# Loads, clears and a bias in the opening stage of a four-layer graph network: x is loaded after the edges' ends, one clear is written at another place, and layer 0's bias is added on DVE

## Chip, core and metric

The kernel runs on one core of a Trainium2 chip. The metric is the device time of one execution in microseconds (us). Three runs of the kernel before gave 7706.85, 7705.21 and 7698.37 us; the median is 7705.21. All profile numbers come from one further execution that the hardware profiler recorded, of 7696.22 us.

## What is computed

A graph has 6250 nodes with 128 features in `x` and 100,000 edges with ends `src` and `dst`, sorted by `dst`. Four layers are applied one after the other, each to a normalised and clipped copy of `x`, and each result is added to `x`. Only layer 0 is touched by the change:

```python
h = jnp.maximum(_layernorm(x, axis=-1), 0.0)
x = x + _L0_gnn_ref(h, edge_index, ...)
# inside layer 0
h = x @ W_w + W_b
row, col = (edge_index[0], edge_index[1])
e = h[row] @ a_src + h[col] @ a_dst + a_b
e = jax.nn.leaky_relu(e, negative_slope=0.01)
attention = jax.nn.softmax(e, axis=0)
out = jax.ops.segment_sum(attention * h[col], row, num_segments=N_NODES)
```

Layers 1 to 3 (a mean over edges, two graph attentions, three edge convolutions) use the same edges and follow later.

## The kernel before, in words

The nodes are held as 49 tiles of 128 rows, the edges as tiles of 128 that are taken in chunks of 512. `tile_gnn_stack` is the opening stage. It ends with a flag (L253) and a branch on it (L255); the fast side of the branch, `stack`, runs the four layers. Nothing of `stack` starts ahead of the branch, so the opening stage and the layers lie one behind the other.

The opening stage has two strands that share the engines:

- **The edges' strand** (L137 to L253). `d_i` and `s_i` are the edges' ends as integers, loaded by L138 on the SP queue and L140 on the ACT queue. DVE turns them into differences, window offsets and masks that are stored to DRAM (`neg_d`, `mk_d`, L189 to L197). PE transposes three of them and DVE copies the results to `srcE`, `dstE`, `endE` (L211, L212). Then 98 steps count how often each node tile occurs: DVE makes a one-hot block `oh` (L230, three buffers), PE adds it up in `pc` (L233), and after each of four parts DVE reduces `pc` to `cnt` and to some limits in `ext` (L236 to L246).
- **The nodes' strand** (`node_steps`, L279 to L357). It is a generator; L235 calls its next step behind each of the 98 counting steps, and L247 runs what is left. It loads the weight `wx`, the bias `bx` and the two halves `av` of the attention vector (L290 to L297, all on the ACT queue), and appends to `wx` and `bx` two columns, their products with `av` (L308, L309). Then each node tile passes through three calls: `norm` (statistics for seven tiles at a time on DVE, L316, L317; a square root on ACT, L319; two small DVE steps, L320, L321; then ACT normalises, L329, PE transposes to `nt`, L331, and ACT copies, L333), `project` (PE: the product with `wx`, L338, and a product of a row of ones with the one-row `bx`, L339, which adds the bias in the accumulator `np`, two buffers) and `keep` (ACT copies `np` to `ev`, four buffers, L345, and its last column to `s_tab`, L346; the SP queue stores `ev` to the table `T0`, L347).

`x` itself is loaded in seven pieces at the top, on the ACT queue (L122 to L124). `clear_rows` (L261 to L269) fills places of a DRAM array with a constant, in two DMAs, one of 9360 KB and one of 195 KB, on the SP queue; for the first part, `rows_d[0]`, it is called at L304, in the nodes' second step. Layer 0's scatters to `rows_d[0]` (L1259) come after the branch.

The code is written in a layer that reorders instructions when the program is built: it keeps data dependencies and decides itself in which order each engine and each DMA queue gets its instructions. Each queue then issues strictly in that order. DMAs from SP and ACT take turns on eight completion semaphores, and a DMA waits until the one that used its semaphore eight DMAs earlier has landed.

Of the kernel before, what the change touches and what calls it, by code (L numbers as in the profile page):

```python
# [8 lines left out]
F32 = mybir.dt.float32  # L9
# [3 lines left out]
OP = mybir.AluOpType  # L13
# [4 lines left out]
P = 128  # L18
N = 6250
NT = 49  # L20
# [8 lines left out]
D = 128  # L29
# [59 lines left out]
def tile_gnn_stack(ctx: ExitStack, tc: tile.TileContext, a: dict, out: bass.AP):  # L89
# [5 lines left out]
    nc = tc.nc  # L95
    V = nc.vector
    const = ctx.enter_context(tc.tile_pool(name="shared", bufs=1))
    ident = const.tile([P, P], F32, name="ident")
# [7 lines left out]
    ones = const.tile([P, P], F32, name="ones")  # L106
# [5 lines left out]
    sh = dict(ident=ident, iof=iof, pid=pid, ones=ones, ones_tail=ones_tail, srcE=srcE, endE=endE)  # L112
# [6 lines left out]
    sh["mk_d"] = mk_d  # L119

    x = const.tile([P, NT, D], F32, name="x")
    xr = a["x"].rearrange("(i p) f -> p i f", p=P)  # L122
    for i in range(0, NT, 7):
        nc.scalar.dma_start(x[:, i:i + 7, :], xr[:, i:i + 7, :])  # L124
    sh["x"] = x
    sh["T0"] = dram.tile([NP, D + 1], F32, name="T0")
    sh["s_tab"] = const.tile([P, NT], F32, name="s_tab")
# [4 lines left out]
    with ExitStack() as st:  # L132
        one = st.enter_context(tc.tile_pool(name="pre", bufs=1))
        work = st.enter_context(tc.tile_pool(name="prew", bufs=3))
        ps = st.enter_context(tc.tile_pool(name="prep", bufs=2, space=PSUM))
        node = node_steps(nc, tc, a, sh, st)
        d_i = one.tile([R, 1024], I32, name="d_i")  # L137
        nc.sync.dma_start(d_i, a["dst"].rearrange("(r j) -> r j", j=1024))  # L138
        s_i = one.tile([R, 1024], I32, name="s_i")
        nc.scalar.dma_start(s_i, a["src"].rearrange("(r j) -> r j", j=1024))  # L140
        edge_i = one.tile([R, 2], I32, name="edge_i")
        V.memset(edge_i[:, 0:1], -1)
        V.memset(edge_i[:, 1:2], 1 << 20)
        dcol = bass.AP(tensor=a["dst"].tensor, offset=a["dst"].offset + 1023,
                       ap=[[1024, R - 1], [1, 1]])
        nc.sync.dma_start(edge_i[1:R, 0:1], dcol)
        dcol = bass.AP(tensor=a["dst"].tensor, offset=a["dst"].offset + 1024,
                       ap=[[1024, R - 1], [1, 1]])
# [41 lines left out]
        for m, src in enumerate((slob, dwb, neg)):  # L190
            for c, at, lo, hi in ((1, 256, 0, 256), (2, 0, 256, 768), (3, 0, 768, 1024)):
                nc.sync.dma_start(bass.AP(tensor=mk_d.tensor,
                                          offset=mk_d.offset + (3 * c + m) * 512 + at,
                                          ap=[[2 * 3 * 512, R], [1, hi - lo]]), src[:, lo:hi])
# [29 lines left out]
        for s in range(len(CAP)):  # L224
            t0, t1 = seg_tiles(s)
            pc = ps.tile([P, 8, NT], F32, name="pc")
            for t in range(t0, t1, 8):
                n = min(8, t1 - t)
# [5 lines left out]
                                 stop=t + 8 >= t1)  # L234
# [26 lines left out]
def clear_rows(nc, rows, none, s):  # L261

    for b0, nb, few in ((0, NT - 1, FEW[s][0]), (NT - 1, 1, FEW[s][1])):
        n = (CAP[s] - few) // P
        nc.sync.dma_start(bass.AP(tensor=rows.tensor, offset=rows.offset + (b0 * CAP[s] + few) * RW,
                                  ap=[[n * RW, P], [CAP[s] * RW, nb], [1, n * RW]]),
                          none[:, None, :n, :].rearrange("p o n f -> p o (n f)")
                          .to_broadcast([P, nb, n * RW]))


def no_rows(nc, pool):

    none = pool.tile([P, 4, RW], F32, name="none")
    nc.vector.memset(none, 0.0)
    nc.vector.memset(none[:, :, D:D + 1], -BIG)
    return none


def node_steps(nc, tc, a, sh, st):  # L279


    V, S = nc.vector, nc.scalar
    x, ident, ones = sh["x"], sh["ident"], sh["ones"]
    one = st.enter_context(tc.tile_pool(name="nd", bufs=1))
    w = st.enter_context(tc.tile_pool(name="ndw", bufs=3))
    ps = st.enter_context(tc.tile_pool(name="ndp", bufs=2, space=PSUM))

    wx = one.tile([P, D + 2], F32, name="wx")
    bx = one.tile([1, D + 2], F32, name="bx")
    nc.scalar.dma_start(wx[:, :D], a["L0_gnn_W_w"])  # L290
    b0 = a["L0_gnn_W_b"]
    nc.scalar.dma_start(bx[:, :D], bass.AP(tensor=b0.tensor, offset=b0.offset, ap=[[0, 1], [1, D]]))
    avs = []
    for j, half in ((0, 1), (1, 0)):
        v = a["L0_gnn_a_w"][half * D:(half + 1) * D, :]
        av = one.tile([P, D], F32, name=f"av{j}")
        nc.scalar.dma_start(av, bass.AP(tensor=v.tensor, offset=v.offset, ap=[[0, P], [1, D]]))  # L297
        avs.append(av)
    eps = one.tile([P, 1], F32, name="eps")
    V.memset(eps, LN_EPS)  # L300
    none = no_rows(nc, one)
    live = {}
    yield
    clear_rows(nc, sh["rows_d"][0], none, 0)  # L304
    for j, av in enumerate(avs):
        for t, n in ((wx, P), (bx, 1)):
            pr = one.tile([n, D], F32, name=f"pr{n}")
            V.tensor_tensor(pr, t[:, :D], av[:n, :], OP.mult)  # L308
            V.tensor_reduce(t[:, D + j:D + j + 1], pr, AX.X, OP.add)  # L309
    yield  # L310

    def stats(g):
        mv = w.tile([P, 7, 2], F32, name="mv")
        for i in range(7):
            s = w.tile([P, 6], F32, name="st")
            V.bn_stats(s, x[:, 7 * g + i, :])  # L316
            V.bn_aggr(mv[:, i, :], s)  # L317
        r = w.tile([P, 7, 2], F32, name="r")
        S.activation(r[:, :, 0], mv[:, :, 1], AF.Sqrt, bias=eps, scale=1.0)  # L319
        V.reciprocal(r[:, :, 0], r[:, :, 0])  # L320
        V.scalar_tensor_tensor(r[:, :, 1], mv[:, :, 0], -1.0, r[:, :, 0], op0=OP.mult, op1=OP.mult)  # L321
        return r

    def norm(i):
        if i % 7 == 0:
            live["r"] = stats(i // 7)
        r = live["r"]
        h = w.tile([P, D], F32, name="h")
        S.activation(h, x[:, i, :], AF.Relu, bias=r[:, i % 7, 1:2], scale=r[:, i % 7, 0:1])  # L329
        pt = ps.tile([P, P], F32, name="nt", bufs=1)  # L330
        nc.tensor.transpose(pt, h, ident)  # L331
        h1 = w.tile([P, P], F32, name="h1")
        S.copy(h1, pt)  # L333
        live[i] = h1

    def project(i):
        pp = ps.tile([P, D + 2], F32, name="np")
        nc.tensor.matmul(pp, live.pop(i), wx, start=True, stop=False)  # L338
        nc.tensor.matmul(pp, ones[0:1, :], bx, start=False, stop=True)  # L339
        live[i] = pp  # L340

    def keep(i):
        pp = live.pop(i)
        ev = w.tile([P, D + 1], F32, name="ev", bufs=4)
        S.copy(ev, pp[:, :D + 1])  # L345
        S.copy(sh["s_tab"][:, i:i + 1], pp[:, D + 1:])  # L346
        nc.sync.dma_start(sh["T0"][i * P:(i + 1) * P, :], ev)  # L347

    for i in range(NT + 2):
        if i < NT:  # L350
            norm(i)
        yield
        if 0 <= i - 1 < NT:
            project(i - 1)
        if 0 <= i - 2 < NT:
            keep(i - 2)
        yield  # L357


# [2008 lines left out]
```

## Time and profile before

| What | Value |
|---|---|
| median of 3 runs | 7705.21 us |
| profiled execution, its span | 7696.22 us, 7694.4 us |
| granted PE clock, mean over the span | 0.902 |
| busy: PE, DVE, ACT, POOL | 6191.9, 4916.1, 2115.0, 5303.9 us |
| opening stage: flag written | 168.39 us after the span's start |
| first DVE work of `stack` | 170.41 us |
| DMA in the first 40 us | 13.76 MB, mean 344 GB/s |

An engine's line in a list of instructions in order of time gives the start, the time of one (or of a merged run, with the count behind an x), engine, line, operation, output and input, and in brackets how long the engine was idle before it and what ended that. SPq and ACTq are DMA issues on the queues of those two engines. PEld is the loading of PE's stationary operand. Times of neighbouring instructions overlap a little, so a pace is read from the distance of two starts. A float32 product takes two passes, and each is counted as an instruction.

### The profile page before, as it was taken

What the parts mean: (1) busy time and instruction counts of PE and PEld (TensorE: products, weight loads), DVE (VectorE), ACT (ScalarE), POOL (GpSimd) and SP (SyncE); (2) the same over time, 40 slices, a digit from 0 to 9 for tenths busy, and PEclk for the clock granted to TensorE, in tenths of its full rate; (3) what the DMA queues carried; (4) which work ended last, traced back from release to release, by engine and by line L of the source; (5) the groups of instructions that cost most, each with busy time, mean ns of one, the idle gap of its engine ahead of it and who ended that gap; (6) DMA issues with size and microseconds to landing.
All of it is one profiled execution on the core that took longest, in us unless ns stands there. A gap on an engine that the chain in (4) does not pass through costs nothing.

```text
span 7694.4 us, 109942 instructions
## 1 busy us (share of the span) xinstructions
PE 6191.9 (80%) x35616; PEld 4418.6 (57%) x35616; DVE 4916.1 (64%) x15100; ACT 2115.0 (27%) x5081; POOL 5303.9 (69%) x5487
## 2 busy tenths in 40 slices
PE   6778886777777999996777777878778887777877
PEld 4677875555555666664554544555555555555554
DVE  5677886444446999995666666555555555555555
ACT  2134556222222222222111123222222222222222
POOL 0777772777776666654777755777767777677776
PEclk7778997999998999998888889999989999899999
DMA  3855763333336455433333324444434444333333
GB/s 121 258 162 168 216 189 124 93 92 93 92 87 133 142 144 146 143 104 95 88 89 93 89 79 125 122 126 122 126 114 123 125 122 126 110 119 118 117 118 108
DMA packets 778747, 954.40 MB, mean 124 GB/s; under 512 B 232584, under 2 KB 552494, under 8 KB 777942
## 3 DMA queue, kind: packets, MB, share of 16 engines
q1 hardware_dynamic: 555332, 519.06, 23.3%
q0 software_dynamic: 187680, 411.54, 18.5%
q10 hardware_dynamic: 35154, 16.67, 0.8%
q8 instruction: 289, 4.73, 0.3%
q14 instruction: 292, 2.39, 0.1%
HBM read 809.79 MB, written 137.02 MB: 123 GB/s over the span
## 4 chain that ended last, share of the span: by engine, by line
PE 39%; DMA 25%; POOL 13%; issue 9%; DVE 9%; ACT 2%; SPq 0%; POOLq 0%; DVEq 0%; ACTq 0%
DMA gb<-TB,srcE 13%; POOL gb L391 6%; PE pa L2011 5%; PE pz L2263 5%; DMA gl<-TLb,srcE 4%; PE pa L2290 4%; DMA g<-T,srcE 3%; PE pm L1892 3%; POOL gl L391 3%; DMA rows_d<-rw,pos 3%; PE pt L2251 3%; POOL g L391 3%; PE pb L2276 2%; PE pt L2253 2%; PE bank L1409 2%
## 5 line engine op out<-in xcount | busy, mean ns | idle before, releaser
L391 POOL DMA_INDIRECT gb<-TB,srcE x2346 | 2246.1, 957 | 859.6 <-issue 650.5
L2265 DVE TENSOR_TENSOR_SCAN sc<-mk,sc,pz 128x512 f32<-128x512 bf16 x585 | 748.4, 1279 | 1123.2 <-PE pz L2263 1123.2
L391 POOL DMA_INDIRECT gl<-TLb,srcE x782 | 783.5, 1002 | 364.4 <-issue 183.2
L391 POOL DMA_INDIRECT gl<-TL,srcE x782 | 754.4, 965 | 360.7 <-issue 153.8
L391 POOL DMA_INDIRECT g<-T,srcE x782 | 740.8, 947 | 357.5 <-issue 165.8
L2253 PE MATMUL pt<-ident,gb 128*128 128x128 f32 x2346 | 487.2, 295 | 608.0 <-DMA gb<-TB,srcE 597.3
L1259 POOL DMA_INDIRECT rows_d<-rw,pos x782 | 776.8, 993 | 251.8 <-issue 174.1
L2253 PEld LDWEIGHTS pt<-ident,gb 128*128 128x128 f32 x2346 | 315.2, 142 | 1051.8 <-DMA gb<-TB,srcE 772.9
L2256 ACT ACTIVATE z<-pt 128x512 f32<-128x512 f32 (+1 forms) x588 | 350.4, 596 | 1678.8 <-PE pt L2253 1571.3
L1897 ACT COPY mT<-pm 128x512 f32<-128x512 f32 (+1 forms) x588 | 343.7, 585 | 1399.0 <-PE pm L1894 1279.5
L1894 PEld LDWEIGHTS pm<-ident,gl 128*128 128x128 f32 x2346 | 317.9, 148 | 634.6 <-issue 318.2
L1892 PE MATMUL pm<-oh,wr 128*128 128x512 f32 (+1 forms) x1176 | 655.7, 641 | 31.6 <-DMA oh<-in_edge_weight 16.1
L2263 PE MATMUL pz<-z,wo 128*128 128x512 f32 (+1 forms) x1176 | 670.4, 655 | 0.0
L2290 PE MATMUL pa<-en,row 128*128 128x128 f32 x4692 | 669.0, 289 | 0.0
L2290 PEld LDWEIGHTS pa<-en,row 128*128 128x128 f32 x4692 | 624.2, 207 | 0.1
L1894 PE MATMUL pm<-ident,gl 128*128 128x128 f32 x2346 | 429.0, 290 | 239.9 <-DMA gl<-TLb,srcE 238.8
L2251 PE MATMUL pt<-oh,wr 128*128 128x512 f32 (+1 forms) x1176 | 612.5, 603 | 0.5 <-DVE ev L2157 0.5
L1898 DVE SCALAR_TENSOR_TENSOR lT<-mT,pm 128x512 f32<-128x512 f32 (+1 forms) x588 | 390.7, 675 | 286.1 <-ACT mT L1897 276.7
L2282 DVE TENSOR_SCALAR en<-iof,endE 128x128 f32<-128x128 f32 x2346 | 550.1, 301 | 0.0
L2276 PEld LDWEIGHTS pb<-ident,sc 128*128 128x128 f32 x2346 | 324.6, 153 | 357.9 <-issue 355.8
L2278 ACT COPY row<-pb 128x512 f32<-128x512 f32 (+1 forms) x588 | 344.1, 585 | 503.9 <-PE pb L2276 502.9
L2011 PE MATMUL pa<-px,oe 128*128 128x260 f32 x1564 | 407.7, 400 | 17.5 <-ACT px L2002 17.5
(346 smaller groups left out, 11735.5 us busy)
## 6 DMA issues: line engine op xcount, KB each, us to landing
mk<-mk_d SPq DMA_DIRECT2D x192, 1024.0 KB
mk<-mk_d SPq DMA_DIRECT2D x96, 512.0 KB
rows<-rows_d SPq DMA_DIRECT2D x98, 390.0 KB
gb<-TB,srcE POOLq DMA_INDIRECT x2346
wr<-TA SPq DMA_DIRECT2D x141, 256.0 KB
rows_d<-none SPq DMA_DIRECT2D x3, 9360.0 KB
ea<-in_edge_attr SPq DMA_DIRECT2D x195, 128.0 KB
wr<-TR SPq DMA_DIRECT2D x47, 448.0 KB
```

The source lines that it names most:

```text
L391: nc.gpsimd.indirect_dma_start(out=dst, out_offset=None, in_=table, in_offset=bass.IndirectOffsetOnAxis(ap=idx, axis=0),)
L1259: ins = nc.gpsimd.indirect_dma_start(out=rows_d[s], out_offset=bass.IndirectOffsetOnAxis(ap=idx, axis=0), in_=src, in_offset=None)
L1892: nc.tensor.matmul(pm[:, c0 * P:], wr[:, fb], oh[:, c0 * P:], start=True, stop=False)
L1894: nc.tensor.matmul(pm[:, c * P:(c + 1) * P], gl[:, c, fb], ident, start=False, stop=c == 3, is_transpose=True)
L2011: nc.tensor.matmul(pg, oe[:, c, :], px[:, c, :], start=c == c0, stop=c == 3)
L2251: nc.tensor.matmul(pt[:, c0 * P:], wr, oh[:, c0 * P:], start=True, stop=False)
L2253: nc.tensor.matmul(pt[:, c * P:(c + 1) * P], gb[:, c, :], ident, start=False, stop=c == 3, is_transpose=True)
L2263: nc.tensor.matmul(pz[:, c0:], wo[conv], z[:, c0:], start=True, stop=True)
L2265: V.tensor_tensor_scan(sc[:, c0:], masks.pop(k)[1][:, c0:], pz[:, c0:], 0.0 if carry[0] is None else carry[0][:, 511:512], OP.add, OP.max)
L2276: nc.tensor.transpose(pb[:, c, :], sc[:, c * P:(c + 1) * P], ident)
L2282: V.tensor_scalar(en[:, c, :], iof, endE[:, t:t + 1], None, op0=OP.is_equal)
L2290: nc.tensor.matmul(pa, row[:, c, :], en[:, c, :], start=c == c0, stop=c == 3)
```

## The change

Three edits, all ahead of the branch:

1. The seven loads of `x` are written behind the loads of `d_i` and `s_i`, still on the ACT queue.
2. The call that clears the places of the first part is taken out of the nodes' second step and written in the loop over the node tiles, at i = 14.
3. The bias `bx` becomes a block of 128 equal rows (loaded by a DMA that repeats the row). The product of ones with `bx` is gone; DVE adds `bx` to `np` and writes `ev`, now with 130 columns. ACT still copies the last column to `s_tab`, now from `ev`. The products with `av` are made for `bx` on 128 rows in place of one.

```diff
@@ tile_gnn_stack
     x = const.tile([P, NT, D], F32, name="x")
-    xr = a["x"].rearrange("(i p) f -> p i f", p=P)
-    for i in range(0, NT, 7):
-        nc.scalar.dma_start(x[:, i:i + 7, :], xr[:, i:i + 7, :])
     sh["x"] = x
...
         s_i = one.tile([R, 1024], I32, name="s_i")
         nc.scalar.dma_start(s_i, a["src"].rearrange("(r j) -> r j", j=1024))
+        xr = a["x"].rearrange("(i p) f -> p i f", p=P)
+        for i in range(0, NT, 7):
+            nc.scalar.dma_start(x[:, i:i + 7, :], xr[:, i:i + 7, :])
@@ node_steps
-    bx = one.tile([1, D + 2], F32, name="bx")
+    bx = one.tile([P, D + 2], F32, name="bx")
     nc.scalar.dma_start(wx[:, :D], a["L0_gnn_W_w"])
     b0 = a["L0_gnn_W_b"]
-    nc.scalar.dma_start(bx[:, :D], bass.AP(tensor=b0.tensor, offset=b0.offset, ap=[[0, 1], [1, D]]))
+    nc.scalar.dma_start(bx[:, :D], bass.AP(tensor=b0.tensor, offset=b0.offset, ap=[[0, P], [1, D]]))
...
-    clear_rows(nc, sh["rows_d"][0], none, 0)
     for j, av in enumerate(avs):
-        for t, n in ((wx, P), (bx, 1)):
-            pr = one.tile([n, D], F32, name=f"pr{n}")
-            V.tensor_tensor(pr, t[:, :D], av[:n, :], OP.mult)
+        for t in (wx, bx):
+            pr = one.tile([P, D], F32, name="pr")
+            V.tensor_tensor(pr, t[:, :D], av, OP.mult)
             V.tensor_reduce(t[:, D + j:D + j + 1], pr, AX.X, OP.add)
...
-        nc.tensor.matmul(pp, live.pop(i), wx, start=True, stop=False)
-        nc.tensor.matmul(pp, ones[0:1, :], bx, start=False, stop=True)
+        nc.tensor.matmul(pp, live.pop(i), wx, start=True, stop=True)
...
-        ev = w.tile([P, D + 1], F32, name="ev", bufs=4)
-        S.copy(ev, pp[:, :D + 1])
-        S.copy(sh["s_tab"][:, i:i + 1], pp[:, D + 1:])
-        nc.sync.dma_start(sh["T0"][i * P:(i + 1) * P, :], ev)
+        ev = w.tile([P, D + 2], F32, name="ev", bufs=4)
+        V.tensor_tensor(ev, pp, bx, OP.add)
+        S.copy(sh["s_tab"][:, i:i + 1], ev[:, D + 1:])
+        nc.sync.dma_start(sh["T0"][i * P:(i + 1) * P, :], ev[:, :D + 1])
...
             keep(i - 2)
+        if i == 14:
+            clear_rows(nc, sh["rows_d"][0], none, 0)
         yield
```

More of the change, by code (lines that the diff above doesn't have):

```diff
@@ L282, in node_steps @@
     V, S = nc.vector, nc.scalar
-    x, ident, ones = sh["x"], sh["ident"], sh["ones"]
+    x, ident = sh["x"], sh["ident"]
     one = st.enter_context(tc.tile_pool(name="nd", bufs=1))
```

## The prediction, made before the changed kernel ran

> **What bounds the kernel now.** I read the chain that ended last first, then the list in order of time up to 171 us, then the table by stretches, the groups of the opening stage, and the built order of both programs.
>
> Chain that ended last, shares of the span by engine:
>
> ```profile
> PE 39%; DMA 25%; POOL 13%; issue 9%; DVE 9%; ACT 2%; SPq 0%; POOLq 0%; DVEq 0%; ACTq 0%
> ```
>
> No engine bounds the whole. But the flag (168.39) and the branch cut the span in two, and all edits lie ahead of the cut, so the opening stage is read by itself. What is saved there moves the rest earlier. In the built programs every engine and queue has the same instructions in the same order behind the branch.
>
> The list in order of time, three stretches of the opening stage:
>
> ```profile
> 5.95 0.40 SPq L265 DMA_DIRECT2D rows_d<-none  x1
> ...
> 32.20 0.69 DVE L186 TENSOR_SCALAR slo<-s_i 98x1024 int32<-98x1024 int32 x1 [12.37 <-DMA s_i<-in_src]
> ...
> 41.37 0.82 ACTq L297 DMA_DIRECT2D av<-in_L_gnn_a_w  x2
> 44.40 0.29 DVE L308 TENSOR_TENSOR pr<-wx,av 128x128 f32<-128x128 f32 x1 [9.60 <-DMA av<-in_L_gnn_a_w]
> ...
> 54.20 0.55 DVE L230 TENSOR_TENSOR oh<-iob,hi 128x392 bf16<-128x392 bf16 x1
> ...
> 142.56 0.51 PE L233 MATMUL pc<-oh,ones_b 128*128 128x392 bf16 x1
> 142.86 0.42 PE L331 MATMUL nt<-ident,h 128*128 128x128 f32 x1
> 143.07 0.64 PE L338 MATMUL np<-wx,h 128*128 128x130 f32 x2
> 143.64 0.80 PE L339 MATMUL np<-bx,ones 1*128 1x130 f32 x2
> 144.37 0.51 PE L233 MATMUL pc<-oh,ones_b 128*128 128x392 bf16 x1
> ...
> 152.75 0.31 ACT L319 ACTIVATE r<-mv,eps 128x7 f32<-128x7 f32 x1
> ```
>
> First DVE waits 12.37 us for `s_i`, which ACT's queue issued behind `x`, and 9.60 us for `av`. Behind that second wait, in DVE's order, stand the copies of `srcE` and all one-hots, so counting starts at 54.20. Then comes the loop over nodes and counts. The starts give PE's pace: pc 0.30, nt 0.21, np 0.57, the bias product 0.73.
>
> The table by stretches (start:end, length, then busy us of PE, PEld, DVE, ACT, POOL, and the granted PE clock):
>
> ```profile
> 80.00:100.00 20.00, 19.97 (x65) 13.40 (x65) 9.22 (x31) 8.89 (x41) 0.00 (x0) 0.50 0.15 41
> 140.00:160.00 20.00, 19.37 (x63) 12.35 (x63) 11.18 (x39) 9.59 (x39) 0.00 (x0) 0.50 0.10 28
> ```
>
> PE fills the loop, at half the clock, and DVE is idle nearly half of it. The square roots (one for seven tiles) start at 57.34 and lastly 152.75: six periods in 95.4 us, 15.9 each. PE's own share of one is 14 counts, 7 transposes, 7 products, 7 bias products: 4.2 + 1.5 + 4.0 + 5.1 = 14.8.
>
> **The change, part by part.**
>
> *The clear.* It does not move. In SP's built order the DMA of 9360 KB is the fifth in both programs, ahead of `neg_d`; only the one of 195 KB goes, from ahead of the stores of `T0` to behind the fourth. I cost this at nothing: it issues in 0.39 us on a queue that has a store each 2 us. And the load of the first `av` still waits for the big clear, whose semaphore it takes over (41.37 is when the clear has landed). Ahead of that the same bytes flow (13.76 MB in 40 us), whichever comes first.
>
> *`x` behind `s_i`.* `s_i` goes first on ACT's queue, beside `d_i`, which DVE reads at 6.70. So the wait of 12.37 us goes. DVE's work up to the first `pr` (10.23 to 19.8, then the five steps of 32.20 to 34.8, then the copies and casts of 45.4 to 54.2) is some 21 us from 10.2, and ends near 31. What is late next is `av`, at 44.40 as before: DVE stands still for 13 us. From there it is 9.8 us ahead, for the first one-hot no longer has the copies between itself and `av`. It gives some back: two statistics that stood at 6.30 now stand here, the products with `av` too (eight steps at 0.2, from 44.40 to 45.40), and two more one-hots ahead of the square root. Counted along the built order, the two small steps L320 and L321 end at 53.0, where before L321 started at 59.66. **A = -6.7** (bounds: 0, should `av` land later by as much; -9.8). The loads of `x` end before 41 and hide under the wait for `av`; without that cover the first statistics would wait for them.
>
> *The bias product goes from PE:* 49 times 0.73 = 35.8 us of an engine that fills the loop. What is left of PE in a period is 9.7 us.
>
> *The add goes to DVE:* 49 times 128x130 from the accumulator. The nearest row is layer 0's last table:
>
> ```profile
> L1530 DVE TENSOR_TENSOR ev<-pp,b1a x49: 252/284/292, 1230.4 to 1319.4; 128x128 f32<-128x128 f32 x49
> ```
>
> 0.284 us; in a run one step starts 0.07 before the last ends (six one-hots of 0.554 take 2.94), so 0.22. A period on DVE: 14 one-hots at 0.49, 7 pairs of statistics at 0.26 (starts 79.98, 80.24), 7 adds, 0.2 for r: 10.4, and a seventh of four `cnt` blocks of 0.9: **10.9 us, more than PE's 9.7.** ACT loses 49 copies of 0.268; it was no bound.
>
> *The new wait.* The add waits for np, and behind it on DVE stand one-hots, which PE counts next; before, this wait was ACT's. I walked one period along the built order, from the start of a block of seven statistics (0): r is ready at 3.8, the first transpose runs at 4.45, the first np ends at 5.83, the next at 7.27, 8.4, 9.5, 10.6. DVE, which reaches its adds at 5.5, 6.7, 8.7, 9.9 and 11.0, stands still for 0.5 and 0.8 us at the first two and not at the others. The next block starts at 11.7; with `cnt`, **12.2 a period**. Bounds: 10.9 with no standing still, and 15.6 if each add waits as ACT's copy of np does now (its group: 33.2 us idle before 49 copies, 0.68 each, 4.7 a period). I take 12.2, since the wait in between is on two engines that are then near balance. Six periods: 73.2 in place of 95.4. **B = -22.2** (-30.0 to -1.8).
>
> *The tail.* From L321 of the last group to the flag is 14.7 us now (153.65 to 168.39), filled by PE. In the walk the last np ends 9.5 after r, and 0.75 later the flag. **C = -4.5** (0 to -6). The store of the last `ev` lands behind it as now: the layers' first DVE step came at 170.41, released by it.
>
> Sum: -6.7 - 22.2 - 4.5 = **-33.4 us**. On the profiled execution's own time, 7696.22, that is 7663; this execution lies 9 us under the median of the three runs, 7705.21, from which I get **7672**. The ends of all terms together: -46 and -2.
>
> **The rivals.** About 0.2%, 15.4 us here, is what a measurement of this kernel can tell from no change.
>
> 1. *PE gets its full clock.* From 77 to 79 us it had it: a count took 0.33 in place of 0.51, np 0.40 in place of 0.64. Then PE's period halves, DVE's 10.9 is all, and the gain is 6.7 + 30 + 6, some 43: 7662. Against it: in the loop the clock stayed at 0.50 from 80 us on, with PE busy 97%; a less busy PE gives no reason for more. The Trainium skill (TensorE: Matmul & The Clock Gate, Part 1) says that sustained activity releases a gated clock within some 3.4 us. By that rule the loop would have run at full clock already, the bias product would be worth about half, and the sum would be nearer -20; the trace disagrees, at 0.50 for 100 us. Chance 0.10.
> 2. *The two engines interlock.* Each add that waits holds up one-hots, PE then lacks counts, and the period becomes 14: -6.7 - 11.4 - 3 = -21, 7684. For it: both engines are strictly in order and near balance, with only three one-hot and two np buffers. Chance 0.17.
> 3. *A wait takes the place of the product.* The adds wait as long as ACT's copies did, 15.6, and `av` lands a few us later because `x` now flows beside the clear: -2 to -12, about 7699. This is also what is left if only the moved bytes count and the rest does not do what it says, as the clear shows. Chance 0.12.
> 4. *Slower, by the clock behind the branch.* PE has 39% of the chain, 3001 us, at a mean granted clock of 0.902. If the shifted start brings it 1% lower (0.893), PE's part costs 30 us and the gain is gone; at 0.887 it is slower by 17 us, about 7722. It decides from 0.892 on. Against it: three runs, each with its own phase, lie within 8.5 us. Chance 0.08.
>
> My forecast, periods of 11.3 to 13.2 us, gains 27 to 39 us: chance 0.53.
>
> **How the numbers follow.** The likeliest case gives 7672. The range goes from 7655 (rival 1, with the 7 us by which the fastest of the three runs lies under the median) to 7699 (rival 3 at its middle). That leaves out rival 4 and half of rival 3, 0.14, and little below. Faster by over 0.2%: the forecast and rivals 1 and 2, 0.80. Within: rival 3, 0.12. Slower: 0.08.
>
> **What would show it.** In the profile after: DVE's wait for `s_i` gone and one of some 13 us for `av` in its place, still ended near 44; the first one-hot at 45; the big clear still issued near 6 us; square roots 12.2 us apart; DVE busy 17 of 20 us in the loop and PE less than now; idle time of DVE before `ev`, released by np, of under 2 us a period; the flag near 135. Wrong would be: `av` landing at another time (A), periods over 14 (B), or a flag at 135 with an unchanged total (rival 4: then the time behind the flag has grown).

## The result, and the profile after

Five runs of the changed kernel gave a median of 7667.68 us (7662.97 to 7673.48). Five runs of the kernel before on the same chip gave 7702.68 (7698.03 to 7706.85). The ratio is 0.9954, with a 95% interval from 0.9943 to 0.9966: 35 us faster. The profiled execution of the changed kernel took 7662.97 us (span 7661.1, mean granted clock 0.907). So the time came out 4 us under the forecast of 7672.

In kernel.py of the changed kernel some lines have other numbers: the square root is L317 (before L319), the product with `wx` L336 (L338), the add that writes `ev` L342, the store of `T0` L344 (L347).

First the chain that ended last, shares of the span by engine:

```profile
PE 37%; DMA 23%; POOL 16%; issue 12%; DVE 9%; ACT 2%; SPq 0%; DVEq 0%; POOLq 0%; ACTq 0%
```

As before, no engine bounds the whole, and the answer lies in the opening stage. The same list in order of time as before (start, time of one, engine, line, operation, and in brackets the idle time before it with what ended that):

```profile
6.20 0.40 SPq L265 DMA_DIRECT2D rows_d<-none  x1
7.90 0.68 DVE L186 TENSOR_SCALAR slo<-s_i 98x1024 int32<-98x1024 int32 x1
...
42.58 0.82 ACTq L296 DMA_DIRECT2D av<-in_L_gnn_a_w  x2
45.76 0.29 DVE L306 TENSOR_TENSOR pr<-wx,av 128x128 f32<-128x128 f32 x1 [15.59 <-DMA av<-in_L_gnn_a_w]
45.98 0.56 DVE L230 TENSOR_TENSOR oh<-iob,hi 128x392 bf16<-128x392 bf16 x1
...
101.11 0.64 PE L336 MATMUL np<-wx,h 128*128 128x130 f32 x2
101.79 0.29 DVE L342 TENSOR_TENSOR ev<-np,bx 128x130 f32<-128x130 f32 x1 [0.73 <-PE np L336]
102.41 0.64 PE L336 MATMUL np<-wx,h 128*128 128x130 f32 x2
103.09 0.29 DVE L342 TENSOR_TENSOR ev<-np,bx 128x130 f32<-128x130 f32 x1 [0.53 <-PE np L336]
104.25 0.29 DVE L342 TENSOR_TENSOR ev<-np,bx 128x130 f32<-128x130 f32 x1
105.34 0.39 PE L336 MATMUL np<-wx,h 128*128 128x130 f32 x2
105.40 0.29 DVE L342 TENSOR_TENSOR ev<-np,bx 128x130 f32<-128x130 f32 x1
...
121.92 0.30 ACT L317 ACTIVATE r<-mv,eps 128x7 f32<-128x7 f32 x1 [2.59 <-DVE mv L315]
132.14 0.16 DVE L253 CAST flag<-pf 128x1 int32<-128x1 f32 x1 [0.48 <-PE pf L252]
134.05 0.49 DVE L274 MEMSET none<- 128x520 f32 x1 [1.75 <-DMA T<-ev]
```

The wait for `s_i` is gone (7.90). One wait for `av` of 15.59 us stands in its place, and the first one-hot follows it at once, at 45.98 in place of 54.20. In the loop, from 78 us on, DVE stands still before the first two adds of each new group of seven tiles (0.73 and 0.53 us here) and before none of the later ones. The flag comes at 132.14.

The table by stretches (start:end, length, busy us of PE, PEld, DVE, ACT, POOL with instructions, the granted PE clock, then the DMA share and GB/s):

```profile
60.00:80.00 20.00, 14.15 (x56) 7.35 (x55) 17.50 (x70) 9.97 (x38) 0.00 (x0) 0.78 0.17 50
80.00:100.00 20.00, 13.53 (x58) 7.12 (x57) 18.88 (x75) 8.52 (x35) 0.00 (x0) 0.84 0.14 40
100.00:120.00 20.00, 16.29 (x67) 9.65 (x68) 17.61 (x63) 10.73 (x41) 0.00 (x0) 0.78 0.15 42
```

The engines have changed places: DVE is now full to 17.5 to 18.9 of 20 us, PE to 13.5 to 16.3. And the granted clock, 0.50 in these stretches before (from 80 us on), is 0.78 to 0.84. The groups of the opening stage, first of the changed kernel (busy us, mean ns of one, then the idle time before the group and what ended it):

```profile
L233 PE MATMUL pc<-oh,ones_b 128*128 128x392 bf16 x97 | 39.5, 422 | 39.1 <-DVE oh L230 38.6
L336 PE MATMUL np<-wx,h 128*128 128x130 f32 x98 | 24.8, 348 | 1.0 <-DVE ev L342 0.5 <-DVE ext L239 0.5
...
L342 DVE TENSOR_TENSOR ev<-np,bx 128x130 f32<-128x130 f32 x49 | 14.0, 286 | 8.3 <-PE np L336 7.5 <-issue 0.5 <-ACT h L331 0.2
```

and of the kernel before:

```profile
L233 PE MATMUL pc<-oh,ones_b 128*128 128x392 bf16 x97 | 46.2, 505 | 8.7 <-DVE oh L230 8.2
L339 PE MATMUL np<-bx,ones 1*128 1x130 f32 x98 | 38.4, 491 | 0.0
L338 PE MATMUL np<-wx,h 128*128 128x130 f32 x98 | 31.2, 420 | 0.0
```

PE now waits 39.1 us for one-hots where it waited 8.7, and yet each of its counts and products has become shorter (422 in place of 505 ns, 348 in place of 420). Nothing in the change touches those instructions. The prediction had argued against this (its first rival, at a chance of 0.10), and the experiments below ask for its cause.

Where the 36 us of the opening stage came from, by the square roots (one per seven tiles) and the flag:

| | before | after | difference | forecast |
|---|---|---|---|---|
| first square root (A) | 57.34 | 51.40 | -5.9 | -6.7 |
| six periods to the last one (B) | 95.4 | 70.5 | -24.9 | -22.2 |
| from there to the flag (C) | 15.6 | 10.2 | -5.4 | -4.5 |
| flag | 168.39 | 132.14 | -36.3 | -33.4 |
| from the flag to the span's end | 7526.0 | 7529.0 | +3.0 | 0 |

### The profile page after: what moved, and what is told of

It reads as the page before. It is cut to its first block, busy times and chain, and to the rows that moved or that the text cites. A ratio compares the mean times of both kernels' runs of the same rounds, so it can differ in the third digit from the quotient of the medians.

```text
span 7661.1 us, 109731 instructions
## 1 busy us (share of the span) xinstructions
PE 6122.6 (80%) x35518; PEld 4358.1 (57%) x35518; DVE 4923.6 (64%) x15149; ACT 2106.4 (27%) x5032; POOL 5308.6 (69%) x5487
## 4 chain that ended last, share of the span: by engine, by line
PE 37%; DMA 23%; POOL 16%; issue 12%; DVE 9%; ACT 2%; SPq 0%; DVEq 0%; POOLq 0%; ACTq 0%
DMA gb<-TB,srcE 11%; POOL gb L390 7%; PE pz L2262 5%; PE pa L2010 4%; POOL gl L390 4%; PE pa L2289 4%; DMA rows_d<-rw,pos 4%; DMA gl<-TLb,srcE 4%; POOL g L390 3%; PE pm L1891 3%; PE pt L2250 3%; DMA g<-T,srcE 3%; PE pb L2275 2%; PE pt L2252 2%; PE pm L1893 2%
## 5 line engine op out<-in xcount | busy, mean ns | idle before, releaser
L2010 PE MATMUL pa<-px,oe 128*128 128x260 f32 x1564 | 404.1, 397 | 17.0 <-ACT px L2001 16.6
```

Source lines behind the costliest of these rows:

```text
L2010: nc.tensor.matmul(pg, oe[:, c, :], px[:, c, :], start=c == c0, stop=c == 3)
```

## The experiments

Theory one at the start: the edits act independently, the clear not at all, and the one-row product costs PE more than its own work because it holds the clock down. The rivals: the edits depend on each other, or the clock follows PE's load alone. The first four kernels ran together on one chip, beside 23 runs of the kernel before (median 7692.47); the next four on another, beside 7 (7699.91); the last four later, told of further down. Times are medians; an opening stage is read from one profiled execution.

| kernel | first square root | us per period | flag | first step of the layers | time, ratio and interval |
|---|---|---|---|---|---|
| before | 57.34 | 15.90 | 168.39 | 170.41 | 7702.68 |
| changed | 51.40 | 11.75 | 132.14 | 134.05 | 7667.68, 0.9954 [0.9943, 0.9966] |
| x load alone | 50.09 | 15.77 | 160.33 | 162.35 | 7683.84, 0.999 [0.998, 1.000] |
| bias on DVE alone | 57.19 | 11.70 | 137.57 | 139.08 | 7672.22, 0.997 [0.9959, 0.9981] |
| clear alone | 56.98 | 15.76 | 167.18 | 169.19 | 7693.73, 1.0001 [0.9992, 1.0011] |
| bias on PE, 128 rows | 57.25 | 9.82 | 125.76 | 128.25 | 7656.08, 0.9956 [0.9939, 0.9972] |
| bias on PE, 32 rows | 57.74 | 13.34 | 153.39 | 155.62 | 7688.91, one run |
| no bias | 58.12 | 9.66 | 124.75 | 128.17 | 7658.22, one run |
| changed, vectors first | 32.24 | 11.93 | 114.32 | 115.71 | 7647.96, 0.9931 [0.9915, 0.9948] |
| changed, clear held back | 36.55 | uneven | 114.77 | 120.44 | 7653.66, 0.9941 [0.9925, 0.9958] |

**1. The x load alone.** The kernel before, with only the first edit:

```diff
-    for i in range(0, NT, 7):
-        nc.scalar.dma_start(x[:, i:i + 7, :], xr[:, i:i + 7, :])
...
         nc.scalar.dma_start(s_i, a["src"].rearrange("(r j) -> r j", j=1024))
+        for i in range(0, NT, 7):
+            nc.scalar.dma_start(x[:, i:i + 7, :], xr[:, i:i + 7, :])
```

> The kernel before with only the first edit: x is loaded behind s_i, the bias stays a one-row product on PE, the clear is called where it was. My theory (three terms that add up, each in its own place): the wait of 12.37 us for s_i goes, the wait for av grows to about 15 us and ends near 45.8, the first one-hot starts near 46, and the loop keeps its period of 15.9 us. Flag some 7 us earlier, near 161 (168.39 before); total -5 to -9 us. Rival (the two edits only pay together: the head start is lost in a loop that PE fills, since PE then waits at the first statistics as before): flag within 2 us of 168, no change in the total.

The first one-hot came at 44.86 and the flag 8.1 us earlier than before; the wait for `av`, 14.53 us, ended at 44.64. The loop kept its period (15.8) and its clock of 0.50. In the total the 8 us are at the edge of what can be told (0.999, from 0.998 to 1.000). So A is a head start and nothing else.

**2. The bias on DVE alone.** The kernel before, with only the third edit of the diff above.

> The kernel before with only the third edit: the bias is a block of 128 rows and DVE adds it; x is loaded first and the clear is called where it was. My theory: first one-hot at 54 as before, square roots 11.8 us apart in place of 15.9, tail 9 in place of 14.7, so the flag near 139; total -27 to -32 us. PE clock in the loop about 0.8. Rival (the head start is what lets DVE run ahead, and without it DVE and PE interlock): periods of 13 and more, flag at 146 or later, total -22 or less.

Flag 30.8 us earlier, 11.70 a period, granted clock 0.75 to 0.91, DVE busy 17.6 to 18.4 of 20 us. The sum of the first two kernels at the flag, -8.1 and -30.8, is -38.9, and both edits together gave -36.3: they are independent but for 2.6 us. The total is another matter: it fell by 20 us (15 to 32 by the interval), less than the 27 to 32 expected and than the 30.8 us at the flag. Why some 10 us are missing there the runs do not show. The forecast's second rival, an interlock at 14 us a period, does not occur.

**3. The clear alone.** The kernel before, with only the second edit.

> The kernel before with only the second edit: the clear of the first part is called at i = 14 of the node loop. My theory: the DMA of 9360 KB still stands fifth on SP and issues near 6 us, only the one of 195 KB moves behind the fourth store; flag within 0.5 us of 168.4, total unchanged within 5 us. Rival (the small DMA at the head of the stores costs, as its 128 rows have to flow ahead of the first table rows): flag 1 to 3 us earlier.

Nothing: 1.0001 (0.9992 to 1.0011). SP's queue shows why. The DMA of 9360 KB still issues fifth, at 5.49 us; only the small one has gone from 45.97 to 68.68, behind four stores of `T0`.

**4. The bias on PE, but on 128 rows.** The kernel before; the row of ones becomes 128 rows, and `bx` holds the bias in row 0 and zeros below, so the sum is the same:

```diff
-    bx = one.tile([1, D + 2], F32, name="bx")
+    bx = one.tile([P, D + 2], F32, name="bx")
+    V.memset(bx, 0.0)
...
-        nc.tensor.matmul(pp, ones[0:1, :], bx, start=False, stop=True)
+        nc.tensor.matmul(pp, ones, bx, start=False, stop=True)
```

The built order of PE, ACT and SP is that of the kernel before, and DVE's differs by the one memset. PE has as many products as before, and each is larger.

> The kernel before, but the bias product takes all 128 rows: a block of ones times a block that holds bx in its first row and zeros below. Same result, same number of PE instructions, same order of work; only the rows of PE's array that the product uses differ. Theory one (the granted clock follows how much of the array is in use, and a one-row product counts as near idle, which is why the loop sat at 0.50 before and near 0.8 after): clock in the loop 0.75 to 1.0, square roots 9 to 13 us apart, flag at 150 or earlier, total -15 us or more. Theory two (the clock follows something else, such as how PE's work is spaced): clock 0.50 as before, periods 15.9, flag within 2 us of 168, total unchanged.

This is the experiment that settles the cause of the faster PE. The stretches of this kernel (up to 64 us of the first one PE still ran at half pace):

```profile
60.00:80.00 20.00, 18.17 (x104) 12.79 (x103) 18.44 (x67) 14.34 (x64) 0.00 (x0) 1.00 0.15 44
80.00:100.00 20.00, 16.34 (x98) 12.71 (x97) 18.77 (x68) 13.58 (x59) 0.00 (x0) 0.87 0.18 51
100.00:120.00 20.00, 16.42 (x103) 12.70 (x102) 18.96 (x68) 13.88 (x60) 0.00 (x0) 0.93 0.17 47
```

and a piece of its list in order of time:

```profile
100.23 0.64 PE L340 MATMUL np<-bx,ones 128*128 128x130 f32 x2
100.67 0.42 PE L332 MATMUL nt<-ident,h 128*128 128x128 f32 x1
...
102.25 0.39 PE L340 MATMUL np<-bx,ones 128*128 128x130 f32 x2
102.48 0.33 PE L233 MATMUL pc<-oh,ones_b 128*128 128x392 bf16 x1
```

PE does 98 to 104 instructions in 20 us where the kernel before did 61 to 65 (from 80 us on), with a granted clock of 0.87 to 1.00 in place of 0.50. And the bias product takes 0.44 us from its start to that of the next instruction while PE runs at half pace (100.23 to 100.67), against 0.73 with one row at the same pace; 0.23 at full pace. The product with `wx` ahead of it takes 0.44 too, against 0.57. These differences, 0.29 and 0.13 us, go with two gaps that the kernel before has in the loading of PE's stationary operand:

```profile
78.51 0.48 PE L339 MATMUL np<-bx,ones 1*128 1x130 f32 x2
78.92 0.49 PE L338 MATMUL np<-wx,h 128*128 128x130 f32 x2
79.34 0.48 PE L339 MATMUL np<-bx,ones 1*128 1x130 f32 x2
...
80.35 0.80 PE L339 MATMUL np<-bx,ones 1*128 1x130 f32 x2
...
143.64 0.50 PEld L339 LDWEIGHTS np<-bx,ones 1*128 1x128 f32 x2 [0.23 <-issue]
144.37 0.10 PEld L233 LDWEIGHTS <-ones_b 128*128 128x128 bf16 x1 [0.23 <-issue]
```

A load for the one-row product, and the load behind it, each stand 0.23 us with nothing that the profile shows to wait for; with 128 rows these gaps are gone and the loads run under the product ahead of them. The first lines show the other half. PE had reached full pace near 77 us, and the second bias product at full pace (79.34) was the last: the next one takes 0.80, and PE stays at half pace to the end of the loop.

The loop is at 9.82 us a period, and DVE, busy 18.4 to 19.0 of 20 us, is what bounds it. Kept on PE in a wider form, the bias is 1.9 us a period cheaper than on DVE (11.70 with the bias on DVE alone), and this kernel, with neither of the other edits, reaches its flag 6.4 us ahead of the changed one. The ratios of the totals, 0.9956 and 0.9954, do not show that lead.

**5. The bias on 32 rows.** As kernel 4, with `ones[0:32, :]` and `bx[0:32, :]`. One run.

> The kernel before, but the bias product takes 32 rows of ones and of a block that holds bx in its first row and zeros below: same result, same order of instructions on every engine. It asks what of the one-row product holds the clock down. Theory one (the share of the array's rows that the loop's products use, averaged): 32 rows are a quarter of the array, so clock 0.5 to 0.7, periods 13 to 16, flag 140 or later. Theory two (any product on less than all 128 rows changes how the rows are loaded, and the change of the row count itself holds PE up): bias product still spaced 0.7 at half clock, clock 0.50, flag near 167. Theory three (only very few rows count as idle): like 128 rows, clock near 0.9, periods 9.8, flag near 126.

It came out in between. Up to 78.70 us PE ran at half pace, as in the kernel before: full pace came only behind the pause after the first group of bias products (77.16 there). With one row it lasted some 3 us, with 32 rows some 27:

```profile
80.00:100.00 20.00, 18.63 (x102) 12.82 (x103) 16.12 (x58) 14.05 (x64) 0.00 (x0) 1.00 0.20 55
100.00:120.00 20.00, 18.86 (x74) 12.79 (x74) 14.73 (x55) 9.55 (x41) 0.00 (x0) 0.65 0.14 38
120.00:140.00 20.00, 18.73 (x60) 11.38 (x60) 11.95 (x42) 8.97 (x37) 0.00 (x0) 0.50 0.11 30
```

With full clock a period takes 10.8 us (83.88, 94.73, 105.57), and then, with the clock at 0.50, 16.1 us, as with one row. The product takes 0.73 at half pace here too (67.94 to 68.67). So the product costs the same beside its neighbours with 32 rows as with one, and yet the full clock is held longer, but not for good. What ended the full clock near 105 us the run does not show.

**6. No bias.** The kernel before without the product; its output leaves the bias of layer 0 out.

> The kernel before without the bias product; nothing adds the bias, so layer 0's table lacks it (ACT copies np as before). It prices the bias by itself. My theory: PE loses the product and its stall and its clock rises to 0.8 or more; DVE has 9.4 us a period and is the fuller engine; periods 9.5 to 10, flag near 125, as with the product on 128 rows (9.8 and 125.76). So the product on 128 rows costs next to nothing, and the add on DVE costs 11.8 - 9.8 = 2 us a period, 14 us in all. Rival (the product on 128 rows still costs PE time that bounds the loop): periods 8.5 or less, flag 117 or earlier.

9.66 us a period, against 9.82 with the 128-row product and 11.70 with the add. This is one execution each, and without the product the layer also put DVE's and ACT's work in a slightly different order. So in a loop that DVE bounds the wide product costs nearly nothing, and the add costs what it takes on DVE (seven of 0.22, 1.5 us) and a part of what DVE stands still for it.

**7. The vectors first.** The changed kernel, with layer 0's weight, bias and attention vectors loaded ahead of `x`, and `x` in five pieces of ten tiles:

```diff
+        next(node)
-        for i in range(0, NT, 7):
-            nc.scalar.dma_start(x[:, i:i + 7, :], xr[:, i:i + 7, :])
+        for i in range(0, NT, 10):
+            nc.scalar.dma_start(x[:, i:min(i + 10, NT), :], xr[:, i:min(i + 10, NT), :])
```

> The changed kernel, with the weights, the bias and both av loaded ahead of x, and x in five pieces in place of seven, so that neither an av nor a piece of x takes over the big clear's semaphore. It tests what the prediction named as late next: DVE's 15.6 us of standing still for av. My theory: first one-hot near 31 in place of 46, first square root near 37, periods 11.8, flag near 119 (the stores of T0 stand behind mk_d on SP until 47, and that costs DVE up to 3 us through the four ev buffers); total 11 to 15 us under the changed kernel. Rival (x itself is late: behind the clear's bytes the first pieces land at 40 or later, and the wait for av turns into one for x): first statistics at 40 or later, gain under 6 us.

The list in order of time:

```profile
2.31 4.18 ACTq L297 DMA_DIRECT2D av<-in_L_gnn_a_w  x2
6.31 0.40 SPq L266 DMA_DIRECT2D rows_d<-none  x1
6.53 21.82 ACTq L141 DMA_DIRECT2D x<-in_x  x5
27.27 0.28 DVE L307 TENSOR_TENSOR pr<-wx,av 128x128 f32<-128x128 f32 x1
27.48 0.56 DVE L231 TENSOR_TENSOR oh<-iob,hi 128x392 bf16<-128x392 bf16 x1
```

`av` issues at 2.31 in place of 42.58, ahead of the clear, and DVE never stands for it: the first one-hot comes 18.5 us earlier, and the flag 17.8 us. The layers' first step stands 18.3 us before that of the changed kernel. By the ratios (0.9931 and 0.9954) the total gains 18 us more than the changed kernel, over the 11 to 15 expected, with intervals that just overlap. The rival, that `x` would then be late, falls.

**8. The clear really held back.** The changed kernel, with both DMAs of the clear made to depend on the add of tile 12, so that the big one cannot be put ahead:

```diff
+        live["add"] = V.tensor_tensor(ev, pp, bx, OP.add)
...
-            clear_rows(nc, sh["rows_d"][0], none, 0)
+            clear_rows(nc, sh["rows_d"][0], none, 0, tc, live["add"])
```

> The changed kernel, with the big clear really moved: both its DMAs are made to depend on the add of tile 12, so that they stand behind the thirteenth store of T0 on SP. It tests what the second edit would have done had the scheduler kept its place. My theory: av no longer waits for the clear and lands near 25, first one-hot near 31, that is 15 us gained; but the clear then issues near 60 and its 9360 KB take some 27 us, the stores of T0 stand behind it on SP's queue (neg_d's issue stood behind it until 33.8 in the changed kernel), the four ev buffers run out after 7 us and DVE stands still for about 20 us: flag 135 to 140, total 3 to 8 us over the changed kernel. Rival (the DMA queue takes the stores beside the clear): flag near 118, total 13 us under the changed kernel.

My expectation was wrong. I had expected DVE to stand still for some 20 us behind the clear, and a time above the changed kernel's. It came out no slower: the ratio is 0.9941 (0.9925 to 0.9958) against 0.9954, with intervals that overlap, and the flag is 17.4 us ahead:

```profile
30.92 0.28 DVE L311 TENSOR_TENSOR pr<-wx,av 128x128 f32<-128x128 f32 x1
...
60.03 21.20 SPq L265 DMA_DIRECT2D rows_d<-none  x2
...
65.55 0.29 DVE L347 TENSOR_TENSOR ev<-np,bx 128x130 f32<-128x130 f32 x1
...
71.69 4.85 DVE L230 TENSOR_TENSOR oh<-iob,hi 128x392 bf16<-128x392 bf16 x10
...
81.33 37.13 SPq L349 DMA_DIRECT2D T<-ev  x36
...
81.41 5.33 DVE L230 TENSOR_TENSOR oh<-iob,hi 128x392 bf16<-128x392 bf16 x11
...
93.78 0.28 DVE L347 TENSOR_TENSOR ev<-np,bx 128x130 f32<-128x130 f32 x1
...
115.53 0.72 DVE L347 TENSOR_TENSOR ev<-np,bx 128x130 f32<-128x130 f32 x2 [0.21 <-DMA T<-ev]
...
120.44 0.49 DVE L279 MEMSET none<- 128x520 f32 x1 [2.74 <-DMA T<-ev]
```

Without the clear ahead of it `av` needs no wait: the first product with it stands at 30.92 in place of 45.76, 14.8 us earlier. And the stores of `T0` did stand behind the clear for 21 us, from 60.03 to 81.33, with no add between 65.55 and 93.78. But the order that the layer built, with the dependence in it, has one-hots there (runs of ten and eleven): DVE was busy 18.6 and 18.9 of 20 us from 60 to 100. The price came at the end. The last five adds stand behind the flag (114.77), some of them waiting for stores, and then the layers' first step waits 2.74 us for the last store. So the flag alone overstates this kernel: at the layers' first step (120.44, against 134.05) it is 13.6 us ahead. That is near the rival's 13, but not for the rival's reason, since the stores did not flow beside the clear.

**9 to 12. The versions together.** Kernel 10 has the x load and the 128-row product. The kernel called e8_best has these and the vectors first. The changed kernel ran again beside them, with 23 runs of the kernel before (median 9249.92); e8_best ran a second time some minutes later, beside 10 (9262.84). Then every version took some 9200 us, with a mean granted clock of 0.83 to 0.84 in place of some 0.90, although the record gives the chip the same number, 8, as that of the first four kernels. The opening stage took what it had taken before (the changed kernel's flag came at 132.14 again); the extra time lies behind the branch, where for instance the costliest group of gathers has the same 2236 us of busy time as in the first run (2250) but 1372 us of idle time in place of 858.

> The kernel before with x loaded behind the edges' ends, as the change does, and with the bias product kept on TensorE but on all 128 rows (128 rows of ones, the bias in row 0 of a block that is zero below); no add on DVE, the clear where it was. Theory one (the head start and the rate of the loop are independent terms): the head start of 8.1 us that the x load alone gave at the flag, and the period of 9.8 us that the 128-row product alone gave. Flag near 125.8 - 8.1 = 117.7, first layer step near 120, granted clock 0.85 to 1.0 from 60 to 110, and 14 us ahead of the changed kernel's flag at 132.1; time about 7645 to 7652 beside a kernel before of about 7695 to 7700, ratio 0.993 to 0.9945, under the changed kernel's 0.9954. Rival (the 128-row product's rate came from the late start, since DVE and ACT had work laid up for it): periods of 11 to 12 us and a flag of 127 to 132, ratio 0.995 to 0.9955, no better than the changed kernel.

> As the kernel before with the x load behind the edges' ends and the bias product on 128 rows, and besides layer 0's weights, bias and attention vectors loaded ahead of x, which comes in five pieces of ten tiles. Theory one (three independent terms): no wait for the attention vectors, first one-hot near 27 to 31, first square root near 32, seven periods of 9.8 us, flag at 101 to 107, first layer step within 3 us of it; time 10 to 14 us under that of the kernel with vectors first and the bias on DVE (7648), so 7634 to 7640, ratio 0.991 to 0.9925. Rival (SP becomes late next: the stores of T0 cannot issue before the masks at 46 us, so the four buffers fill and ACT, which now evicts the product, stands): a stall at the first evictions up to about 47, flag at 110 to 116, time no better than 7646. Second rival (the clock falls back to 0.50 in the loop): periods of 14 to 16 us, flag above 125.

> The changed kernel itself again, beside the two kernels above on one chip, so that the versions are compared on the same runs. Both theories expect what it gave before: ratio 0.9943 to 0.9966 against the kernel before, flag within 1.5 us of 132.1, square roots 11 to 12.5 us apart.

> The same kernel as e8_best, run once more because the chip it met took some 9200 us for every version. The trace of the opening stage is expected as it was there: square roots 9.7 us apart, flag at 101 to 102, first layer step near 104. If what lies behind the branch takes the 7524 to 7530 us that it took for the kernel before and the changed one on the first chip, the time is 7635 to 7640, ratio 0.991 to 0.9925. Rival (a shorter opening stage is given back behind the branch, as the 128-row kernel's 11 us were not to be seen in the total of the slower chip): 7650 to 7668, ratio 0.9935 to 0.9955, no better than the changed kernel or the one with vectors first.

| kernel | first square root | us per period | flag | first step of the layers | time, ratio and interval |
|---|---|---|---|---|---|
| e10_x_and_128 | 50.56 | 9.98 | 119.98 | 123.08 | 9211.54, 0.9957 [0.9941, 0.9973] |
| e8_best | 33.16 | 9.66 | 101.25 | 104.24 | 9185.21, 0.9931 [0.9906, 0.9955] |
| after_again | 51.29 | 11.77 | 132.14 | 134.29 | 9210.59, 0.996 [0.9944, 0.9976] |
| e8_again | 33.70 | 9.77 | 102.38 | 105.20 | 9198.56, 0.9924 [0.9903, 0.9945] |

In the opening stage the terms nearly add up, as theory one had it (kernel 10's flag at 119.98, expected at 117.7): from the changed kernel, 12.2 us at the flag for the product in place of the add, and another 18.7 for the vectors. The rival on the stores' buffers shows, but small. In e8_best:

```profile
33.16 0.30 ACT L321 ACTIVATE r<-mv,eps 128x7 f32<-128x7 f32 x1
...
40.50 0.27 ACT L347 COPY ev<-np 128x129 f32<-128x129 f32 x1
...
45.80 10.19 SPq L349 DMA_DIRECT2D T<-ev  x14
...
48.09 0.27 ACT L347 COPY ev<-np 128x129 f32<-128x129 f32 x1 [1.77 <-DMA T<-ev]
...
101.25 0.16 DVE L254 CAST flag<-pf 128x1 int32<-128x1 f32 x1 [0.47 <-PE pf L253]
```

After four copies the buffers are full; SP issues the first store at 45.80, behind the masks, and the fifth copy runs at 48.09. Only the second period is longer for it (11.2 us, the others 8.6 to 9.9).

The totals of that occasion cannot tell kernel 10 from the changed one: 0.9957 and 0.996, each with an interval of 0.0016 to either side, which is 15 us, while 12 us were at stake. Kernel 10's 0.9957 also lies above the 0.993 to 0.9945 that were expected of it. From the flag to the span's end one execution of kernel 10 took 9102 us and one of the changed kernel 9066, so what follows the branch moves by more than that from run to run. e8_best is faster than the kernel before in both (0.9931 and 0.9924); against the changed kernel beside it its lead is 25 us by the medians, and all six of its runs lie below all twelve of the changed kernel's, although the two intervals overlap.

## Why the prediction was right

**The clear: right.** The big DMA stayed fifth in SP's order, and alone the edit gives 1.0001.

**A, right, with one size off.** DVE's second wait did end near 44, and the first one-hot did follow it at once. It gained 5.9 and not 6.7 us because that wait ended 1.4 us later (45.76, not 44.40), while the work from there to the end of L319 took 8.1 us and not the 8.6 that were counted. `av` issued at 42.58, not at 41.37. The trace bears out what it waits for: on the semaphore of that issue the clear's last landing stands at 41.35 us before and at 42.56 after, each 0.02 us ahead of the issue. With the x load alone the wait ended at 44.64, with the bias alone at 44.23, so neither edit makes it as late by itself; a second execution of the changed kernel gave 45.64, and why both edits together do it stays open. "Late next" was the right question: kernels 7 and 8, each in its own way, take away that wait and gain 17.8 and 17.4 us at the flag, half as much as the whole change (18.3 and 13.6 at the layers' first step).

**B, right by the walk, although one of its reasons failed.** 24.9 in place of 22.2 us. The forecast took 10.9 us of DVE work a period and 1.3 us of standing still. Measured were 11.75: 8.3 us of idle time before 49 adds, 1.2 a period, and so some 10.6 of work. So the mis-sized term is DVE's own work, by 0.3 us.

What failed is the sentence against the first rival, "a less busy PE gives no reason for more". The clock rose to 0.78 to 0.84, and kernel 4 shows that PE's load alone is not what sets it: with the same order of instructions and larger products it rose to 0.87 and more. The one-row product kept it down. That rival's time, 7662, lay 10 us under the forecast, and the result in between. DVE bounds the period at 10.9 in both, and what the higher clock could still save was the waits. It saved little of them, because PE now stands idle for one-hots ahead of each block of seven and falls back to half pace: the first four products of the period at 100 us took 0.64 each, the later ones 0.39 to 0.46. So the walk, made at half pace throughout, had nearly the right stalls (0.5 and 0.8 us; 0.73 and 0.53 measured). That is in part luck: nothing in the prediction said that PE would be at half pace just there and at full pace behind.

Before the run, the Trainium skill (TensorE: Matmul & The Clock Gate, Part 1) was set aside with the trace's 0.50 for 100 us. The runs give it more room. Continuous work of full-row products brought full pace after 4.5 to 7.0 us (a run of counts began at 51.33, 57.18 and 58.05, and the first product with `wx` of 0.39 to 0.41 us stands at 57.66, 64.18 and 62.56, in the changed kernel, with 128 rows and without bias). In the kernel before itself PE came to full pace at 77.16, 5.2 us after the last one-row product of a group had ended (71.98). That section of the Trainium skill gives one busy window of some 3.4 us, which does not begin with the work; the times here are one to about two such windows and do not contradict it. But with one-row products among its work, from 62 to 72 us, PE stayed at half pace, in a stretch in which it was busy 97% of the time (19.41 of the 20 us from 60 to 80): what the Trainium skill calls activity cannot be busy time alone. From 60 to 77 us the column of the granted clock reads 1.00 while a product with `wx` takes 0.64, because the records of the clock begin only with the first change, at 76.7 us; so the pace is to be read from the durations, and from the column only where both agree.

**C, right, some 1 us short** (-5.4 in place of -4.5, or -5.6 from the small step L319, which the forecast counted from).

**The other rivals.** The interlock would have shown as 14 us a period; 11.70 and 11.75 were measured. A wait in place of the product would have left 15.6. Behind the flag the time grew by 3.0 us in one execution, far from the 30 of the fourth rival; between the occasions this part moved by 20%, more than by any edit here.

**Where a larger gain went.** The third edit removed 36 us of PE work and put 11 us of adds on the engine that then bounds the loop, and gained 31 us at the flag. All that it won there, and 12 us more, can be had with the product left on PE: the wide form gained 42.6 us at the flag (kernel 4), against 43.6 for no bias at all (kernel 6). In the totals, kernel 4 lies 16 us under the bias on DVE alone, which ran beside it (7656.08 and 7672.22).

## What to carry to other kernels

When an engine fills a loop, look at what a cheap instruction does to those beside it before moving it to another engine: here a product of one row cost more through the pace it held PE at, and the gaps around it, than through its own work, and the same product on 128 rows cost 0.16 us a period in a loop that DVE bounds. Move work only to an engine with room left in the same period, and count its period first. And of a load that is "late next", ask which transfer its issue waits for: an order of loads that cost nothing brought, at the flag, half as much again as the whole change.

## What the runs showed of the hardware

- The pace of PE depends on how many rows its products use. With one order of instructions, one row gave a granted clock of 0.50 with a bias product of 0.73 us; 32 rows gave half pace, then 1.00 for some 27 us and then 0.50, with the same 0.73 at half pace; 128 rows gave 0.87 to 1.00, with 0.44 at half pace and 0.23 at full. What the gate measures (the rows, or something that comes with them), and why the 32-row kernel lost its clock near 105 us, stays open.
- The granted clock was low also where PE waited for one-hots, with no bias product at all: 0.59 and 0.56 in kernel 8 in the two stretches from 60 to 100 us, with PE busy 14.9 and 16.6 of 20 us.
- A weight load for a one-row product, and the load behind it, each stood 0.23 us at half pace with no wait that the profile shows; with 128 rows neither did.
- A load whose completion semaphore was last used by a DMA of 9360 KB waits for that one to land: `av`, of 64 KB, issued at 42.58 us, 0.02 us behind the clear's last landing, and at 2.31 or 19.60 us where it was ahead of the clear or the clear came later.
- On one occasion all versions took 20% longer, at a mean granted clock of 0.84 in place of 0.90, and none of that lay in the opening stage; what caused it is not known.
